# Centring the attention weights once instead of the tokens, and mask and residual of the last image on VectorE

## The chip, the core and the metric

The kernel runs on one core of a Trainium2 chip. The metric is the device time of one execution in microseconds, the median of the runs; lower is better. Five engines work side by side, each through its own list of instructions, in order: TensorE (PE, with its weight loads shown apart as PEld), VectorE (DVE), ScalarE (ACT), GpSimd (POOL), and SyncE (SP), which here only issues DMA transfers. An instruction that waits for another engine holds up everything behind it on its own engine.

## The reference

Four images of 384 channels and 32 x 32 pixels go through two layers. All of it is float32.

```python
# layer 0: x + conv(groupnorm(x)); four directional scans, merged, layer norm, gelu
x = x + _L0_conv_ref(_gn(x), ...)
t = _to_tokens(x)                                   # (4, 1024, 384)
t = t + _L1_attn_ref(_ln_t(t), Wq, Wk, Wv)          # causal attention, one head of 384
t = t + _L1_ffn_ref(_ln_t(t), gate_w, ..., b2)      # 4 experts, the best 2 count

def _ln_t(v, eps=1e-5):
    m = jnp.mean(v, axis=-1, keepdims=True)
    s = jnp.var(v, axis=-1, keepdims=True)
    return (v - m) / jnp.sqrt(s + eps)
```

The attention is softmax(q k^T / sqrt(384)) v with q, k and v linear in the normed tokens. A mean taken off the tokens can therefore be taken off the weights: with J the matrix that averages over channels, (v - m) W equals v (I - J) W.

## The kernel before, in words

Channels lie on the 128 partitions in M = 3 groups, tokens along the free dimension (L = 1024). An image is worked off in two stages.

*Scan stage.* Image b has 192 units (`IMAGE`), 768 over the four images. A unit is one selective scan over 1024 tokens on 128 partitions: ACT makes `da` by an exponential (L551), DVE multiplies `v` = du x B (L558) and runs the scan `h` (L564), POOL multiplies `h` by C (L571), and every four units PE sums them into `y` (L596, "row"). For part of image 0, `v` comes from PE instead (L841).

*Token stage.* When the last row of an image is in, `evict` (L616) forms `yb`, and `finish` does a layer norm on it (`layernorm`, names ending in `l0`), the gelu (L857) and the residual (L862). Then `behind` runs `attention` and `experts`. Attention loads two weights, wg = Wq Wk^T scaled (made once by `fold` after image 0 and kept in DRAM as `g_d`) and wv, norms the tokens to `axn`, and makes `qt` (pq, L896) and `vt` (pv, L907). For every block of 128 queries it then makes `scores` (ss, L925, with the causal mask added by an identity matmul, L930), `softmax` (L939 to L955), `turn` (transposes tp, L970) and, for every two blocks, `values` (po, L991, with the residual `yb` added by an identity matmul, L988). A copy by ACT brings the result back into `yb` (L1003), and a DMA stores it. `experts` is 8 rounds (two halves of the tokens, four experts) of 36 + 36 float32 matmuls of 512 columns, ph (L1182) and fy (L1207); the profile counts each float32 matmul as two instructions.

*What sets the order.* The program is written out by hand, tick by tick. The last loop of the kernel gives one unit to each tick, up to tick 767, and goes on without units until all is done. Within a tick the order is: functions that are due (`defer`), `v` of this tick's unit (`front`), POOL's product (`back`), functions due `inner`, then one step of every parked generator (`unpark`), then the scan (`middle`), then `go_on`. In `go_on` the generators in `side` (`fold`, `finish`, the norms ahead of the experts) may each go on by about one microsecond's worth of PE work, and then the first of `waiting` (attention and experts of one image) as far as a budget reaches: `pace` microseconds are added to `spare` in each tick, 4.4 in attention and 3.3 in the experts, and every yield of `"pe", n` takes n off. `"wait", n` pauses a generator for n ticks, and `"inner"` moves it ahead of the scan of the next tick. Matmul results go to PSUM banks handed out by `banks` (four of them), and buffers of one image row to `slots` (eight).

*The attention's layer norm* in `layernorm` (L626 to L705, names ending in `at`): PE takes the mean with the full `mean_w` (mu, L639), which leaves it on all partitions; DVE subtracts it (L652) from `yb` into `axn`; ACT squares (L664); PE averages the squares with 32 columns of `mean_w`, four blocks of 128 tokens side by side in the array (var, L671); ACT takes the root (L679), DVE the reciprocal (L684), PE spreads it over the partitions (rb, L690), and DVE multiplies (L700). `axn` lies in pool `a0`, which has one buffer: the accumulator of the experts of the image before (`fx`) lies there too, so the subtraction waits until that image is `stored`.

In ticks: image 0's rows end so that `finish` starts at tick 195, `fold` is done at 204, the attention begins at 206 and its norm is over at 210. Image 1: attention from 398, experts of image 0 written out by 396. Image 2: from 590, norm over at 595, experts of image 1 written out by 589. Image 3: from 782, experts of image 2 written out by 780.

Of the kernel before, what the change touches and what calls it, by code (L numbers as in the profile page):

```python
# [8 lines left out]
F32 = mybir.dt.float32  # L9
AF = mybir.ActivationFunctionType  # L10
ALU = mybir.AluOpType
# [4 lines left out]
P = 128  # L16
B = 4
# [32 lines left out]
def hybrid_kernel(  # L50
# [120 lines left out]
        for b in range(B) for h in range(NH)  # L171
    }
    g_d = dram.tile([P, M, C], F32, tag="g", name="g_d")


    def load_image(b):
# [446 lines left out]
            waiting.append(behind(b))  # L623


    def layernorm(dst, src, name, lag, b=0, into=None):  # L626

# [6 lines left out]
        for h in range(n):  # L636
# [4 lines left out]
                )  # L641
            mus.append(mu)
            yield "pe", 2.6
        if into is not None:
            while b > 0 and b - 1 not in stored:

                yield "wait", 1
            dst = into()
        yield "inner", 0
        for h in range(n):  # L650
            s = bass.ts(h, 512)
# [46 lines left out]
        for h in range(n):  # L698
# [3 lines left out]
                ALU.mult,  # L702
            )
            banks.give(f"rb_{name}_{h}")
        return dst  # L705

    folded = []

    def fold():

        def square(name):
            t = pools["ht"].tile([P, M, L], F32, tag="ht", name=name)
            t = t.rearrange("p m l -> p (m l)")[:, : 2 * M * C]
            return t.rearrange("p (j c d) -> p j c d", j=2, c=M)

        raw = square("w_raw")
        for j, w in enumerate((wq, wk)):  # L720
            nc.sync.dma_start(raw[:, j], w.rearrange("(c p) d -> p c d", p=P))
        wt = square("w_t")
        yield "wait", 2
        for j in range(2):
            for d in range(M):
                ps = yield from banks.take(f"pwt_{j}_{d}")
                for c in range(M):
                    nc.tensor.transpose(
                        ps[:, c * P : (c + 1) * P], raw[:, j, c, d * P : (d + 1) * P], ident
                    )  # L730
                yield "wait", 1
                nc.scalar.copy(wt[:, j, d, :], ps[:, :C])
                banks.give(f"pwt_{j}_{d}")
        g = square("g_s")[:, 0]
        for m in range(M):
            ps = yield from banks.take(f"pg_{m}")
            for d in range(M):
                nc.tensor.matmul(
                    ps[:, :C], wt[:, 0, d, m * P : (m + 1) * P], wt[:, 1, d, :],
                    start=(d == 0), stop=(d == M - 1),  # L740
                )
            yield "wait", 1
            nc.scalar.activation(g[:, m, :], ps[:, :C], AF.Copy, scale=-scale)
            banks.give(f"pg_{m}")
        yield "wait", 1
        nc.sync.dma_start(g_d, g)
        folded.append(1)


# [97 lines left out]
    def finish(b):  # L847
# [8 lines left out]
        for m in range(M):  # L856
# [9 lines left out]

            defer(1 + m // 2, add)

    def attention(b, yb, fx0):
        while not folded:  # L870
            yield "wait", 1
        gw_ = []
        for name, w in ((f"wg_{b}", g_d), (f"wv_{b}", wv.rearrange("(c p) d -> p c d", p=P))):
            ta = yield from slots.take(f"{name}a", P, 2, C)
            nc.sync.dma_start(ta, w[:, :2, :])
            tb = yield from slots.take(f"{name}b", P, C)
            nc.sync.dma_start(tb, w[:, 2, :])
            gw_.append((ta[:, 0, :], ta[:, 1, :], tb))
        xn = yield from layernorm(
            None, yb, f"at_{b}", 0, b,  # L880
            lambda: pools["a0"].tile([P, M, L], F32, tag="a0", name=f"axn_{b}"),
        )
        qt = pools["ht"].tile([P, M, L], F32, tag="ht", name=f"qt_{b}")
        vt = pools["ht"].tile([P, L // P, C], F32, tag="ht", name=f"vt_{b}")

# [33 lines left out]
        def scores(i):  # L919
            ss = []  # L920
            for o in range(0, (i + 1) * P, 512):
                e = min((i + 1) * P, o + 512)
                ps = yield from banks.take(f"ss_{b}_{i}_{o}")
                for c in range(M):
                    nc.tensor.matmul(  # L925
                        ps[:, : e - o], qt[:, c, i * P : (i + 1) * P], xn[:, c, o:e],
                        start=(c == 0), stop=(c == M - 1 and e <= i * P),
                    )
                if e > i * P:
                    nc.tensor.matmul(ps[:, e - o - P : e - o], ident, causal, start=False, stop=True)  # L930
                ss.append((o, e, ps[:, : e - o]))
                yield "pe", 2.6 * (e - o) / 512
# [2 lines left out]

        def softmax(i, ss, pr):
            nb = sm.tile([P, 4], F32, tag="nb", name=f"nb_{b}_{i}")
            for n, (o, e, ps) in enumerate(ss):
                nc.vector.tensor_reduce(nb[:, n : n + 1], ps, AX.X, ALU.min)  # L939
            if len(ss) == 2:  # L940
# [38 lines left out]
        def values(step):  # L979
# [3 lines left out]
            for m in range(M):  # L983
# [1 line left out]
                    names.append(f"po_{b}_{step}_{m}")  # L985
                    po = yield from banks.take(names[-1])
                pv = po[:, (m % 2) * TQ : (m % 2 + 1) * TQ]
                nc.tensor.matmul(pv, ident, yb[:, m, s], start=True, stop=False)  # L988
                for j in range(nj):
                    o = max(0, j - 2 * step) * P  # L990
                    nc.tensor.matmul(  # L991
                        pv[:, o:], vt[:, j, m * P : (m + 1) * P], pts[step][j // 4][:, j % 4, o:],
                        start=False, stop=(j == nj - 1),
                    )
                if m % 2 == 0:
                    pos.append(po)
# [3 lines left out]
            def add():  # L1000
                for m in range(0, M, 2):
                    n = min(2, M - m)
                    nc.scalar.copy(  # L1003
                        yb[:, m : m + n, s],
                        pos[m // 2][:, : n * TQ].rearrange("p (m t) -> p m t", m=n),
                    )
                banks.give(*names)
                nc.sync.dma_start(t2_d[b][:, :, s], yb[:, :, s])
                if step == 1:
# [389 lines left out]
```

## Time and profile before

| | |
|---|---|
| median of 3 runs | 3795.2 us (3794.46 to 3797.17) |
| the profiled execution | 3795.0 us, of which the span of the profile is 3793.2 us |
| mean granted clock of TensorE | 0.927 |
| DVE busy / PE busy / ACT busy | 2964.4 / 3366.5 / 2089.9 us |
| last scan ends | 3121.8 us |
| first pq matmul of the last image | 3186.6 us |
| first expert matmul of the last image | 3283.4 us |

Up to about 3122 us the scans of the four images run, from about 690 us on with the attention and the experts of the image before beside them on PE. From 3122 us on only the last image's token stage is left, behind the rest of image 2's experts. Times in a timeline are microseconds from the span's start; in brackets stands the idle time of the engine ahead of the instruction and what ended it.

### The profile page before, as it was taken

The numbers are of one execution on the slowest core, as the hardware profiler recorded it, in microseconds if no ns is written. First come the engines' busy times: TensorE is split into PE (matmuls) and PEld (weight loads), VectorE is DVE, ScalarE is ACT, GpSimd is POOL, SyncE is SP. The second block draws the span as 40 slices with busy tenths as digits, with TensorE's granted clock in tenths as the row PEclk, the third lists the DMA queues.
The fourth block names the chain that finished last, engine by engine and source line by source line (L and its number), as shares of the span: only waits on it lengthen the run. The fifth ranks groups of instructions, "written<-read, shape, count | busy, mean of one in ns | idle before, by whom it ended". The sixth has DMA issues, their size and how long they took to land.

```text
span 3793.2 us, 34275 instructions
## 1 busy us (share of the span) xinstructions
PE 3366.5 (89%) x11543; PEld 1518.3 (40%) x11543; DVE 2964.4 (78%) x2084; ACT 2089.9 (55%) x2767; POOL 1815.1 (48%) x776
## 2 busy tenths in 40 slices
PE   4666666689999999799999999889999999999999
PEld 1333333245333334345333343354343434644444
DVE  6899899998889999989998999999999982210000
ACT  5888888555656656556655555455554552422121
POOL 2777777554455556445555565455665550000000
PEclk7767877799999999898999999899999999999999
DMA  6655655635576767336666565345656551222321
GB/s 207 218 209 219 220 199 208 230 122 184 191 245 208 255 205 251 140 136 225 215 221 223 197 212 185 143 167 195 215 194 237 180 182 38 91 78 80 96 83 53
DMA packets 407983, 678.80 MB, mean 179 GB/s; under 512 B 33488, under 2 KB 280576, under 8 KB 407808
## 3 DMA queue, kind: packets, MB, share of 16 engines
q1 hardware_dynamic: 401600, 676.22, 52.0%
q8 instruction: 91, 1.49, 0.2%
q10 hardware_dynamic: 6208, 0.39, 0.1%
q14 instruction: 84, 0.69, 0.1%
HBM read 604.57 MB, written 71.96 MB: 178 GB/s over the span
## 4 chain that ended last, share of the span: by engine, by line
DVE 42%; PE 40%; ACT 7%; issue 6%; DMA 3%; POOL 1%; DVEq 0%; SPq 0%; POOLq 0%; ACTq 0%
DVE h L564 25%; PE ph L1182 13%; PE fy L1207 13%; DVE v L558 12%; PE y L596 4%; ACT da L551 2%; PE ss L925 2%; PE pq L896 2%; PE pv L907 2%; PE v L841 1%; PE pxd L391 1%; ACT st L819 1%; DVE du L438 1%; DMA du<-dts 1%; PE po L991 1%
## 5 line engine op out<-in xcount | busy, mean ns | idle before, releaser
L571 POOL TENSOR_TENSOR h<-h,bc 128x1024 f32<-128x1024 f32 x768 | 1814.0, 2366 | 1308.6 <-DVE v L558 1142.8
L564 DVE TENSOR_TENSOR_SCAN h<-da,v 128x1024 f32<-128x1024 f32 x768 | 1750.5, 2284 | 104.4 <-PE v L841 29.7
L551 ACT ACTIVATE da<-dt,a 128x1024 f32<-128x1024 f32 x768 | 883.3, 1156 | 923.7 <-DVE h L564 887.2
L1182 PE MATMUL ph<-fx,w 128*128 128x512 f32 x2304 | 1024.8, 601 | 6.5 <-ACT dt L430 2.3
L1207 PE MATMUL fy<-ht,w 128*128 128x512 f32 x2304 | 1021.2, 600 | 1.5 <-ACT dt L430 0.9
L558 DVE TENSOR_TENSOR v<-du,bc 128x1024 f32<-128x1024 f32 x678 | 841.7, 1241 | 38.8 <-DMA du<-dts 21.7
L1182 PEld LDWEIGHTS ph<-fx,w 128*128 128x128 f32 x2304 | 434.9, 192 | 583.4 <-issue 528.9
L1207 PEld LDWEIGHTS fy<-ht,w 128*128 128x128 f32 x2304 | 436.8, 192 | 574.9 <-issue 552.2
L596 PE MATMUL y<-h,sel 128*32 128x512 f32 x3072 | 493.8, 661 | 101.4 <-POOL h L571 101.3
L1167 ACT ACTIVATE ht<-ph,b1s 128x512 f32<-128x512 f32 x384 | 257.2, 678 | 459.5 <-PE ph L1182 459.1
L1216 DVE SCALAR_TENSOR_TENSOR fy<-fy,b2s,tw 128x512 f32<-128x512 f32 x96 | 72.4, 754 | 425.8 <-PE fy L1207 425.8
L596 PEld LDWEIGHTS y<-h,sel 128*32 128x32 f32 x3072 | 97.4, 116 | 412.2 <-issue 219.8
L841 PE MATMUL v<-ident,st 128*128 128x128 f32 x720 | 143.1, 364 | 110.6 <-DVE h L564 110.6
L819 ACT ACTIVATE st<-turn,bt 128x128 f32<-128x128 f32 x736 | 213.6, 532 | 0.1
L841 PEld LDWEIGHTS v<-ident,st 128*128 128x128 f32 x720 | 115.4, 189 | 155.6 <-DVE h L564 78.3
L1171 ACT ACTIVATE ht<-ht 128x3072 f32<-128x3072 f32 x64 | 176.9, 2763 | 0.8
L551 ACT ACT_TABLE_LOAD x108 | 138.6, 1283 | 13.8 <-DMA dt<-dts 11.9
L991 PE MATMUL po<-pt,vt 128*128 128x256 f32 x480 | 105.4, 368 | 9.4 <-ACT pt L887 9.4
L424 PE MATMUL pdt<-xd,wdt 12*128 12x512 f32 x184 | 81.0, 762 | 34.8 <-ACT dt L430 19.4
L925 PE MATMUL ss<-axn,qt 128*128 128x512 f32 (+3 forms) x288 | 106.1, 514 | 0.8 <-ACT pr L943 0.5
L991 PEld LDWEIGHTS po<-pt,vt 128*128 128x128 f32 x480 | 93.1, 195 | 24.9 <-ACT pt L887 12.0
L939 DVE TENSOR_REDUCE nb<-ss 128x1 f32<-128x512 f32 (+3 forms) x48 | 26.1, 554 | 78.8 <-PE ss L930 63.5
(200 smaller groups left out, 1661.7 us busy)
## 6 DMA issues: line engine op xcount, KB each, us to landing
bc<-rows SPq DMA_DIRECT2D x384, 512.0 KB, 4.9
w<-in_w SPq DMA_DIRECT2D x384, 384.0 KB, 6.1
dt<-dts SPq DMA_DIRECT2D x192, 512.0 KB, 3.8
du<-dts SPq DMA_DIRECT2D x192, 512.0 KB, 6.7
dts<-dt SPq DMA_DIRECT2D x48, 512.0 KB, 5.3
dts<-du SPq DMA_DIRECT2D x48, 512.0 KB, 3.8
fx<-t2d SPq DMA_DIRECT2D x12, 768.0 KB, 5.3
tw<-mkd SPq DMA_DIRECT2D x32, 256.0 KB, 6.3
```

The source lines that it names most:

```text
L551: nc.scalar.activation(u["da"], spread["dt4", n], AF.Exp, scale=a4[:, g, u["q"] : u["q"] + 1])
L558: return nc.vector.tensor_tensor(u["v"], spread["du4", n], spread["bc", n][:, 0, :], ALU.mult)
L564: nc.vector.tensor_tensor_scan(u["h"][:, ::step], u["da"][:, ::step], u["v"][:, ::step], 0.0, op0=ALU.mult, op1=ALU.add,)
L571: product = nc.gpsimd.tensor_tensor(h, h, spread["bc", n][:, 1, :], ALU.mult)
L596: nc.tensor.matmul(y, sel, h, start=first, stop=last, tile_position=(0, jj * DJ))
L819: nc.scalar.activation(st[:, 4 * h + t, :].rearrange("p (d i) -> p i d", i=NI)[:, i, :], ps[h][:, t * P : (t + 1) * P], AF.Copy, scale=bt[ ...
L841: nc.tensor.transpose(u["v"][:, t * P : (t + 1) * P], st[:, t, u["j"] * P : (u["j"] + 1) * P], ident)
L925: nc.tensor.matmul(ps[:, : e - o], qt[:, c, i * P : (i + 1) * P], xn[:, c, o:e], start=(c == 0), stop=(c == M - 1 and e <= i * P),)
L991: nc.tensor.matmul(pv[:, o:], vt[:, j, m * P : (m + 1) * P], pts[step][j // 4][:, j % 4, o:], start=False, stop=(j == nj - 1),)
L1167: nc.scalar.activation(ht[:, f, :], ps, AF.Identity, bias=bias)
L1182: nc.tensor.matmul(ps, tiles[n][:, c, (f % 2) * P : (f % 2 + 1) * P], xns[h][:, c, :], start=(c == 0), stop=(c == M - 1),)
L1207: nc.tensor.matmul(pss[m], tiles[n][:, f, :], hts[fh][:, f, :], start=(fh == 0 and f == 0), stop=(fh == 1 and f == FH - 1),)
```

## The change

Four parts. (1) `fold` centres the three weights: two small matrices, `centre[1]` = I - J's own block and `centre[0]` = the block beside it, take the place of the identity in the transposes, so that each block of a transposed weight is a sum of three matmuls; wv is loaded, centred by nine matmuls, and kept in DRAM as `wv_d`. (2) The attention's norm becomes `scaled_tokens`: squares and means are taken of the tokens as they are, both means with the 32-column form, the variance is the difference, and only one multiplication from `yb` into `axn` is left. The wait for `stored` moves behind the statistics. (3) For the last image (`alone`) DVE adds the mask to the scores in PSUM in place of PE's identity matmul. (4) For the last image DVE adds the attention's result onto `yb`, in place of PE's identity matmul and ACT's copy.

```diff
     def fold():
+        extra = pools["a0"].tile([P, M, L], F32, tag="a0", name="w_extra")
+        extra = extra.rearrange("p m l -> p (m l)")
+        vs = extra[:, : 2 * M * C].rearrange("p (j c d) -> p j c d", j=2, c=M)
+        centre = extra[:, 2 * M * C : 2 * M * C + 2 * P].rearrange("p (j d) -> p j d", j=2)
+        nc.sync.dma_start(vs[:, 0], wv.rearrange("(c p) d -> p c d", p=P))
+        for same in range(2):
+            nc.vector.scalar_tensor_tensor(
+                centre[:, same, :], ident, float(same), mean_w, ALU.mult, ALU.subtract
+            )
...
                 for c in range(M):
-                    nc.tensor.transpose(
-                        ps[:, c * P : (c + 1) * P], raw[:, j, c, d * P : (d + 1) * P], ident
-                    )
+                    for o in range(M):
+                        nc.tensor.matmul(
+                            ps[:, c * P : (c + 1) * P], raw[:, j, o, d * P : (d + 1) * P],
+                            centre[:, int(o == c), :], start=(o == 0), stop=(o == M - 1),
+                        )
...
         nc.sync.dma_start(g_d, g)
+        for m in range(M):
+            ps = yield from banks.take(f"pwv_{m}")
+            for c in range(M):
+                nc.tensor.matmul(
+                    ps[:, :C], centre[:, int(c == m), :], vs[:, 0, c, :],
+                    start=(c == 0), stop=(c == M - 1),
+                )
+            yield "wait", 1
+            nc.scalar.copy(vs[:, 1, m, :], ps[:, :C])
+            banks.give(f"pwv_{m}")
+        yield "wait", 1
+        nc.sync.dma_start(wv_d, vs[:, 1])
         folded.append(1)
...
+    def scaled_tokens(b, yb):
+        sqs = []
+        for c in range(M):
+            sq = yield from slots.take(f"sq_at_{b}_{c}", P, L)
+            nc.scalar.activation(sq, yb[:, c, :], AF.Square)
+            sqs.append(sq)
+        var = yield from banks.take(f"var_at_{b}")
+        for o, src in ((NH * P, [yb[:, c, :] for c in range(M)]), (0, sqs)):
+            for h in range(NH):
+                for c in range(M):
+                    for q in range(4):
+                        k = h * 512 + q * P
+                        nc.tensor.matmul(
+                            var[32 * q : 32 * (q + 1), o + h * P : o + (h + 1) * P],
+                            mean_w[:, :32], src[c][:, k : k + P],
+                            start=(c == 0), stop=(c == M - 1), tile_position=(0, 32 * q),
+                        )
+                yield "pe", 1.0
+        slots.give(*[f"sq_at_{b}_{c}" for c in range(M)])
+        rs = one.tile([P, NH, P], F32, tag=f"rs{NH}", name=f"rs_at_{b}")
+        flat = rs.rearrange("p h t -> p (h t)")
+        nc.scalar.activation(flat, var[:, NH * P : 2 * NH * P], AF.Square)
+        yield "inner", 0
+        nc.vector.tensor_tensor(flat, var[:, : NH * P], flat, ALU.subtract)
+        banks.give(f"var_at_{b}")
+        nc.scalar.activation(rs, rs, AF.Sqrt, bias=eps)
+        yield "wait", 1
+        nc.vector.reciprocal(rs, rs)
+        backs = []
...
+        while b > 0 and b - 1 not in stored:
+            yield "wait", 1
+        xn = pools["a0"].tile([P, M, L], F32, tag="a0", name=f"axn_{b}")
+        yield "inner", 0
+        for h in range(NH):
+            s = bass.ts(h, 512)
+            nc.vector.tensor_tensor(
+                xn[:, :, s], yb[:, :, s], backs[h].unsqueeze(1).to_broadcast([P, M, 512]), ALU.mult
+            )
+            banks.give(f"rb_at_{b}_{h}")
+        return xn
...
     def attention(b, yb, fx0):
+        alone = b == B - 1
...
-        xn = yield from layernorm(
-            None, yb, f"at_{b}", 0, b,
-            lambda: pools["a0"].tile([P, M, L], F32, tag="a0", name=f"axn_{b}"),
-        )
+        xn = yield from scaled_tokens(b, yb)
...
-                if e > i * P:
+                if e > i * P and not alone:
                     nc.tensor.matmul(ps[:, e - o - P : e - o], ident, causal, start=False, stop=True)
...
         def softmax(i, ss, pr):
+            if alone:
+                ps = ss[-1][2][:, -P:]
+                nc.vector.tensor_add(ps, ps, causal)
...
-                nc.tensor.matmul(pv, ident, yb[:, m, s], start=True, stop=False)
+                if not alone:
+                    nc.tensor.matmul(pv, ident, yb[:, m, s], start=True, stop=False)
...
-                    nc.scalar.copy(
-                        yb[:, m : m + n, s],
-                        pos[m // 2][:, : n * TQ].rearrange("p (m t) -> p m t", m=n),
-                    )
+                    y, po = yb[:, m : m + n, s], pos[m // 2][:, : n * TQ]
+                    po = po.rearrange("p (m t) -> p m t", m=n)
+                    if alone:
+                        nc.vector.tensor_add(y, y, po)
+                    else:
+                        nc.scalar.copy(y, po)
```

In the attention the second weight is read from `wv_d` instead of `wv`.

## The prediction

> **What bounds the kernel now.** I read the page's busy times and slices first, then the engines' shares by stage, then the timeline around the three places that the change touches.
>
> ```profile
> PE 3366.5 (89%) x11543; PEld 1518.3 (40%) x11543; DVE 2964.4 (78%) x2084; ACT 2089.9 (55%) x2767; POOL 1815.1 (48%) x776
> DVE  6899899998889999989998999999999982210000
> ...
> 2346.60:3130.40 783.80, 745.28 (x2549) 324.24 (x2548) 740.61 (x508) 411.09 (x436) 447.54 (x190) 0.97 0.54 185
> 3130.40:3186.60 56.20, 47.69 (x213) 22.87 (x213) 24.55 (x20) 14.97 (x20) 0.00 (x0) 0.94 0.19 64
> 3217.60:3283.40 65.80, 64.91 (x331) 49.01 (x329) 13.61 (x31) 27.10 (x59) 0.00 (x0) 1.00 0.18 59
> 3283.40:3793.20 509.80, 503.73 (x1218) 225.16 (x1217) 45.05 (x83) 117.54 (x125) 0.00 (x0) 0.99 0.27 82
> ```
>
> The last four lines give span, then busy time of PE, PEld, DVE, ACT, POOL, the granted clock and DMA. The first is image 3's scan stage: DVE 740.6 of 783.8 us. The rest is mostly gaps of 0.1 us, so DVE sets the pace; PE looks as busy, but a unit costs DVE 3.69 us, plus about 0.23 for the experts' sums (24 pairs of 0.75 + 0.69 in some 150 ticks), against 3.3 + 0.46 us of PE work per tick. The second is the start of the tail, where PE has holes, the others the last attention and experts, where PE runs with hardly a gap. So the time is DVE's up to 3122 us, the latency of a norm up to 3187, PE's from there on.
>
> Prices, with count, sum and mean in ns, then the idle time ahead:
>
> ```profile
> L652 DVE TENSOR_TENSOR axn<-yb,mu_at 128x1536 f32<-128x1536 f32 x8 | 13.7, 1749 | 3.9 <-DMA out<-fx 3.9
> L930 PE MATMUL ss<-causal,ident 128*128 128x128 f32 x64 | 12.3, 274 | 0.0
> L988 PE MATMUL po<-yb,ident 128*128 128x256 f32 x96 | 29.7, 391 | 1.0 <-ACT pr L943 0.8 <-ACT pt L887 0.2
> L728 PE MATMUL pwt<-ident,w_raw 128*128 128x128 f32 x18 | 3.6, 341 | 1.7 <-ACT w_t L732 1.5 <-DMA w_raw<-in_wq 0.2
> ```
>
> And the last image's norm on PE, then DVE:
>
> ```profile
> 3159.90 5.32 PE L1207 MATMUL fy<-ht,w 128*128 128x512 f32 x12
> 3166.55 5.97 PE L639 MATMUL mu_at<-yb,mean_w 128*128 128x512 f32 x12 [1.34 <-DVE yb L862]
> 3176.57 3.30 PE L671 MATMUL var_at<-sq_at,mean_w 128*32 128x128 f32 x48 [4.04 <-ACT sq_at L664]
> 3182.84 3.59 PE L690 MATMUL rb_at<-rs_at,ident 128*128 128x128 f32 x16 [2.98 <-DVE rs_at L684]
> 3186.57 1.98 PE L896 MATMUL pq<-axn,wg_3a 128*128 128x512 f32 x4
> ...
> 3174.09 3.42 DVE L652 TENSOR_TENSOR axn<-yb,mu_at 128x1536 f32<-128x1536 f32 x2 [3.93 <-DMA out<-fx]
> ```
>
> From `yb` complete (3168.8) to the first pq pass 17.8 us, of which DVE waits until 3174.1 for the store of image 2, whose buffer `axn` takes.
>
> **What the Trainium skill says.** "Perfetto Trace Analysis", Identifying the Most-Contended Engine, warns that matmul busy time says little of how near PE is to its limit. The trace agrees: matmul records overlap (mean 600 ns for ph), so I price PE by spacing: 72 ph passes in 30.90 us of the chain are 0.43 us each, a 128-column pass is 0.11 (two L930 passes: 0.22), a 256-column one 0.22 (two of L988: 0.43). "VectorE: DVE Perf Modes", The TRN2 errata, gives (N+151)/0.96 ns for a float32 tensor_tensor; the trace has 1749 to 1754 for N = 1536 (formula 1757) and 687 for 512 (691). I use it as an estimate where no row exists: 0.42 us for N = 256, 0.29 for 128. "TensorE: Matmul & The Clock Gate", Why this matters for your kernels, says PE-idle gaps over about 3 us halve the clock; above, 48 var passes took 3.30 us after a 4.04 us gap, while 24 of the same form took 0.86 in a busy stretch. "ScalarE: Activation LUTs", What ACT_TABLE_LOAD costs, puts a table load at 1283 ns; the page shows 1283.
>
> **Part 1, the norm in images 0 to 2 (beside scans).** DVE loses two subtractions (3.41 us back to back) and gains one of 256 columns, 0.42: -2.99. Its new wait: squares and 96 passes must be through by then. In images 1 and 2 `spare` is 3.3 when the norm begins, so four yields of 1.0 push the rest into the next tick and the subtraction comes two ticks on; no wait. In image 0 `spare` is 4.4, it comes one tick on: da 1.15 + three squares of about 1.05 (from 619 ns for 512 columns) + var's end 0.8 + square 0.47 = 5.6 us against DVE's 4.9 of scan and products, so 0.7 us of waiting, with the scan and with it POOL and `da` queued behind. Sum -2.3 - 3.0 - 3.0 = -8.3. PE loses 12 passes of 0.43 and gains 48 in 1.6: -3.6 per image, beside DVE's work, so worth nothing there. In image 2 the buffer wait leaves the front of the norm, which ends after 4 ticks instead of 5: the experts are written out by tick 779 instead of 780.
>
> **Part 2, fold.** PE: 54 matmuls of two 128-column passes, 11.9 us, for 18 one-pass transposes, 2.0; plus 9 matmuls of two 384-column passes (pg: six in 1.93 us), 5.8. Together +15.7 us between 687 and 747 us. There PE's idle pieces (the timeline's brackets, such as 4.46 us before var_l and 3.71 within a row) sum to 18 us, which covers it. ACT gets three copies of 0.49, DVE two small operations, +0.6. SP gets wv's load ahead of `w_raw`'s two (0.59 MB, about 3 us at 200 GB/s), which the first pwt waits for, with mu_l and the row behind it on PE; DVE's first subtraction of that norm now starts 6.7 us after mu_l ends, and its multiplication 2.2 us after rb_l. I put the stalls at +1.5, bounds 0 (all covered) and 18.7 (work and load laid bare). `folded` comes at 208 instead of 204, the attention two ticks later, its norm a tick shorter, so experts 0 end at 397, within the 398 at which image 1 begins; beyond that each tick would cost up to 3.7 us. The read of `wv_d` right behind its write holds SP perhaps 4 us, with fetches behind it that lead by 3 ticks (11 us) and land in 3.8 to 6.7: covered.
>
> Scan stage: -8.3 + 0.6 + 1.5 = **-6.2** (bounds 0 and -12, as the DVE's present waits for a late PE, up to 5.4 us each, shift either way when token work moves a tick against the rows).
>
> **Part 3, start of the tail.** Counted from the last row's end (3130.3 before, pq 56.3 later). With experts 2 a tick earlier, the budget gives PE this order: fy 5.15, mu_l 5.15, fy 5.15, var_l 1.6, fy 5.15, half rb_l 0.9, fy 5.15, half rb_l 0.9: 29.2, against 29.8 before, but the last fy now lies inside the chain, not behind it. DVE then has an fy pair 1.45 and the last multiplications: 33.2; table load and gelus +4.8 = 38.0; residual 39.3. PE is cold by then (10 us idle): mean passes 3.3 and var 2.9 = 45.5, subtraction 45.9, root (its table loaded meanwhile) 46.4, reciprocal 48.2, first half rb 50.0, first multiplication 51.8. That is 4.5 less. One more ph group ahead of the row may delay it by 1.5: **-3.0** (bounds +3, all of that group and a late reciprocal; -8, if PE stays warm). The store no longer matters; it ends before the multiplication.
>
> **Part 4, last attention.** PE loses 8 masks of 0.22 and 12 identities of 0.43: -6.96. DVE gets 8 x 0.29 and 4 x (0.69 + 0.42) against 13.6 us busy in 65.8, ACT loses its copies. But the mask waits for the last score block, and stands before the reductions of both: a softmax of two blocks is ready 0.6 to 0.8 us later. Before values of step 2, PE already waits 0.90 us for `pt` behind that softmax on ACT; there the gain of 0.65 turns to a loss of 0.4, and three smaller spots lose about 0.3 each: +1.9. **-5.1** (bounds -7.0 and -2). The experts behind it are PE at full rate and only shift.
>
> **Sum.** -6.2 - 3.0 - 5.1 = -14.3 on the profiled execution's 3795.0 us (span 3793.2 and 1.8 around it; the median, 3795.2, is 0.2 off): 3780.7, so **3781 us**.
>
> **Rivals.** (A) The forecast, own range 3773 to 3787; for it, DVE's continuous stretches. (B) Scan stage gives nothing: what DVE saves it waits for PE (the timeline has waits of 4.9 us for mu_ff and 5.4 for ss). 3795.0 - 3.0 - 5.1 = 3787. Against it: in 2880 to 3090 us DVE hardly waits. (C) More: waits shrink too, PE stays warm: -9 - 6.5 - 6.5 = 3773. Against it: the idle PE above. (D) Slower: fold. If PE's cover of 18 us is mostly not where the passes fall, the laid-bare 18.7 us plus one tick of 3.7 for image 1 and one of 3.7 for image 2 outweigh 16.4 of gains (14.3 with the 0.6 + 1.5 of fold's cost put back): 3795.0 + 26.1 - 16.4 = 3805. It decides from 16.4 us of fold's cost. For it: rows and mu_l stand behind pwt in PE's order; against it: seven buffers of h let scans run ahead of rows.
>
> **Numbers.** A 0.56, B 0.22, C 0.12, D 0.10. A measurement of this kernel can tell 0.2%, 7.6 us, from no change. B lies at that edge and splits. Faster: 0.53 + 0.12 + 0.11 = 0.76; same: 0.03 + 0.11 + 0.02 = 0.16; slower 0.08. Range 3769 to 3792 leaves out D and the ends of C and B.
>
> **What would show it.** Last scan ends near 3116 us instead of 3121.8; PE's first pq of image 3 some 9 us earlier than 3186.6, the first ph some 14 earlier than 3283.4, equal passes after it. Around 690 to 750 us no new DVE wait over 2 us for mu_l, rb_l or du. Wrong would be: a last scan at or behind 3122, experts of image 0 running into image 1's norm, or PE waiting for `pt` more than 4 us in the last attention.

## The result and the profile after

| | before | after |
|---|---|---|
| median of 8 runs, us | 3796.18 (3790.32 to 3803.41) | 3781.78 (3778.22 to 3784.2) |
| profiled run, us (its span) | 3795.0 (3793.2) | 3782.19 (3780.4) |
| last scan ends | 3121.8 | 3114.3 |
| last `y` pass ends | 3130.35 | 3125.58 |
| first pq pass of image 3 | 3186.57 | 3176.97 |
| first ph pass of image 3 | 3283.44 | 3272.45 |

The ratio of after to before is 0.9965 (95% interval 0.9956 to 0.9974): faster by 0.35%, about 13 us (the two medians lie 14.4 us apart). The forecast was 3781 us.

The stages of the changed kernel, in the columns used before (window and length, then busy time of PE, PEld, DVE, ACT and POOL, the granted clock, and DMA):

```profile
2342.40:3125.60 783.20, 743.75 (x2597) 327.17 (x2595) 738.50 (x507) 414.35 (x436) 447.63 (x190) 0.97 0.55 185
3125.60:3177.00 51.40, 38.70 (x237) 21.95 (x237) 21.73 (x19) 15.01 (x18) 0.00 (x0) 0.85 0.21 69
3208.90:3272.50 63.60, 60.40 (x292) 43.96 (x290) 19.20 (x47) 23.58 (x51) 0.00 (x0) 0.97 0.19 61
3272.50:3780.40 507.90, 501.96 (x1217) 223.98 (x1217) 45.06 (x83) 117.55 (x125) 0.00 (x0) 1.00 0.28 82
```

The first window is image 3's scan stage up to the last row. DVE is busy 738.5 of 783.2 us, as full as before; the stage's length is compared below by counting scans, since the left edge of this window is put by hand. The second is the start of the tail, 4.8 us shorter. The third is the last attention, where TensorE's busy time fell from 64.9 to 60.4 us but 3.2 us of idling stand beside it and the clock is 0.97, not 1.00. The fourth, the experts, is 1.8 us shorter although the same passes run in it: in before its clock was 0.99.

The start of the tail on TensorE in the timeline of the changed kernel (start, duration, then in brackets the idle time ahead and what ended it):

```profile
3147.86 1.05 PE L686 MATMUL rb_l<-rs_l,ident 128*128 128x128 f32 x8
...
3153.90 1.05 PE L686 MATMUL rb_l<-rs_l,ident 128*128 128x128 f32 x8
3160.95 0.66 PE L902 MATMUL var_at<-yb,mean_w 128*32 128x128 f32 x8 [6.00 <-DVE yb L881]
...
3166.32 2.54 PE L902 MATMUL var_at<-sq_at,mean_w 128*32 128x128 f32 x48
3173.07 3.76 PE L922 MATMUL rb_at<-rs_at,ident 128*128 128x128 f32 x16 [4.21 <-DVE rs_at L917]
3176.97 2.83 PE L968 MATMUL pq<-axn,wg_3a 128*128 128x512 f32 x4
```

One group of fy passes (5.32 us) stands between the two halves of rb_l. The second half is late, so TensorE idles 6.00 us, and 48 var passes then take 2.54 us; the second line of windows has a mean granted clock of 0.85 for this stretch. The norm's DVE work is what was priced: the subtraction takes 0.42 us, each of the two multiplications 1.75.

### The profile page after: what moved, and what is told of

The parts are those of the page before. It is cut to its first block, busy times and chain, and to the rows that moved or that the text cites. A ratio compares the mean times of both kernels' runs of the same rounds, so it can differ in the third digit from the quotient of the medians.

```text
span 3780.4 us, 34707 instructions
## 1 busy us (share of the span) xinstructions
PE 3348.6 (89%) x11755; PEld 1523.6 (40%) x11755; DVE 2962.4 (78%) x2098; ACT 2088.0 (55%) x2754; POOL 1815.4 (48%) x776
## 5 line engine op out<-in xcount | busy, mean ns | idle before, releaser
L997 PEld LDWEIGHTS ss<-axn,qt 128*128 128x128 f32 x288 | 50.5, 193 | 50.2 <-issue 30.0
```

What stands on the lines that cost most here:

```text
L997: nc.tensor.matmul(ps[:, : e - o], qt[:, c, i * P : (i + 1) * P], xn[:, c, o:e], start=(c == 0), stop=(c == M - 1 and (alone or e <= i * P)),)
```

## How to compare scan stages

The table counts from the start of the 101st scan, which comes at 380.1 to 386.1 us from run to run although the program up to there is the same everywhere; that drift belongs to no change. "Scans" is the time from there to the start of the last scan; the three columns behind it are the stages of 192 scans that carry the tokens of images 0, 1 and 2; then come three stretches of the tail: "row to pq" from the end of the last `y` pass (the row) to the first pq, "ss to ph" from the first score pass to the first expert pass, and "experts" from there to the end.

| kernel | scans | im. 0 | im. 1 | im. 2 | row to pq | ss to ph | experts | span |
|---|---|---|---|---|---|---|---|---|
| before | 2738.6 | 831.2 | 823.9 | 783.8 | 56.2 | 65.8 | 509.8 | 3793.2 |
| after | 2728.7 | 828.5 | 820.2 | 780.5 | 51.4 | 63.6 | 508.0 | 3780.4 |
| e1_fold_only | 2741.1 | 824.0 | 832.0 | 785.5 | 63.0 | 65.8 | 509.7 | 3806.1 |
| e2_norms_012 | 2728.8 | 828.7 | 820.0 | 780.6 | 55.3 | 65.8 | 509.7 | 3787.1 |
| e3_norms_all | 2728.9 | 828.8 | 819.9 | 780.5 | 51.3 | 65.8 | 509.7 | 3781.6 |
| e4_alone_only | 2735.9 | 829.0 | 823.1 | 784.1 | 56.5 | 61.9 | 508.1 | 3787.5 |
| e5_fold_double | 2736.2 | 835.8 | 819.8 | 781.0 | 51.1 | 63.6 | 508.0 | 3785.0 |
| e6_mask_late | 2728.7 | 825.7 | 820.8 | 782.5 | 51.4 | 61.0 | 511.3 | 3780.1 |
| e7_late_and_copies | 2728.9 | 828.9 | 819.9 | 780.5 | 51.3 | 60.1 | 507.9 | 3776.1 |
| e8_fold_3_ticks | 2736.4 | 826.7 | 827.1 | 783.0 | 50.8 | 63.6 | 507.9 | 3784.3 |
| e9_wait_front | 2731.5 | 828.0 | 820.5 | 783.3 | 48.4 | 63.6 | 507.9 | 3773.9 |
| e10_residual_only | 2736.1 | 830.7 | 821.8 | 781.1 | 51.1 | 62.4 | 509.7 | 3787.8 |
| e11_all | 2725.6 | 825.3 | 820.0 | 780.6 | 48.7 | 59.2 | 509.6 | 3774.1 |
| e12_fold_light | 2725.9 | 825.7 | 820.9 | 779.6 | 51.1 | 63.6 | 507.9 | 3775.3 |

Up to the last scan seven of these are the same program (after, e2, e3, e6, e7, e10, e11). They show what one profile can tell: the scans lie between 2725.6 and 2736.1 us, image 0 between 825.3 and 830.7, image 1 between 819.9 and 821.8, image 2 between 780.5 and 782.5. Before and e4 are one program as well. A difference below some 10 us in the scans, 5 us in image 0, or 2 us in images 1 and 2, is therefore read from no single profile, and the differences of scan stages below are to be taken with that spread.

## The experiments

**The parts put in one after the other.** The first three kernels rebuild the change in steps; the fourth is its last step alone on the kernel before. Centring twice gives the same as once, so the old norm can stand beside the new weights.

```diff
 # e1_fold_only (e2: the new norm "if b in (0, 1, 2)"; e3: in all images)
-        alone = b == B - 1
+        alone = False
-        xn = yield from scaled_tokens(b, yb)
+        xn = yield from centred_norm(None, yb, f"at_{b}", 0, b, lambda: ...)  # as in before
```

> The fold of the change alone: centred weights, but the norm of all four images as before (centring tokens that no longer need it changes nothing in what is computed), mask and residual on TensorE as before. Theory (the prediction's term): fold costs +2.1 us in all, the last scan ends at 3121.8 + 2.1 = 3123.9 us, ratio to before 1.0006. Rival (fold laid bare, the case in which the forecast would have been slower): +16 to +26, last scan at 3138 or later, ratio 1.004 to 1.007. A second rival (its work is all beside DVE): last scan within 1 us of 3121.8.

> Fold and the new norm in images 0 to 2; image 3 keeps the old norm, mask and residual on TensorE. Theory (additive savings of DVE work): last scan 8.3 us earlier than with the fold alone, near 3115.6, and a tail as before behind it; ratio 0.9984. Rival (part of the saving becomes waiting for PE, as the trace of the changed kernel suggests by its new waits of 6.0 and 7.7 us for du in image 0): image 0 keeps at most 2 us of its saving, the last scan comes only 5 to 7 us earlier than with the fold alone. If all of it became waiting (case B of the prediction), it would stand where the fold alone leaves it.

> The changed kernel with mask and residual of the last image left on TensorE: all four norms new. Theory: same last scan as with images 0 to 2 alone, from the last row's end to the first pq pass of image 3 51.8 us instead of 56.3, and from that pq to the first ph pass 96.9 us as in the kernel before; ratio 0.9976. Rival: the gain of the tail's start is eaten by PE standing one group of expert passes further behind the rows (the y evict waits 11 us and not 8.6), so that pq comes only 2 us earlier than with the old norm.

> The kernel before with the last image's mask and residual added by DVE, nothing else. Theory (the prediction's Part 4): first pq to first ph 91.8 us instead of 96.9, the time 5.1 us less, ratio 0.9987; scan stage unchanged to the tick. Rival (from the changed kernel's trace, where this stretch took 95.5): new waits of PE for pt and for the norm's reciprocal behind the residual on DVE give most back; 94 to 96 us, ratio 0.9992 to 0.9997.

| kernel | median, us | ratio to before (95%) |
|---|---|---|
| e1_fold_only | 3807.5 | 1.0033 (1.0020 to 1.0045) |
| e2_norms_012 | 3788.19 | 0.9982 (0.9976 to 0.9989) |
| e3_norms_all | 3785.17 | 0.9975 (0.9966 to 0.9985) |
| e4_alone_only | 3791.47 | 0.9990 (0.9982 to 0.9998) |

The fold alone makes the kernel slower by 12 us, between the first expectation and the second, and far from the third. Its scans take 2.5 us more than in before and 5.2 more than in e4. That this lies near the +2.1 confirms nothing: equal programs spread further, and the reckoning put the cost into image 0, where e1 takes 824.0 us, less than before and e4 do, while image 1 takes 832.0, some 8 us more. In the profile's 12.9 us there are also 3.2 of the drift ahead of the 101st scan. The tail has 6.8 (row to pq 63.0 instead of 56.2). Its timeline on TensorE:

```profile
3134.11 1.92 PE L597 MATMUL y<-h,sel 128*32 128x512 f32 x16
3135.97 5.42 PE L1344 MATMUL ph<-fx,w 128*128 128x512 f32 x12
...
3165.59 15.62 PE L1369 MATMUL fy<-ht,w 128*128 128x512 f32 x36
3181.04 5.31 PE L715 MATMUL mu_at<-yb,mean_w 128*128 128x512 f32 x12
...
3199.06 2.47 PE L1052 MATMUL pq<-axn,wg_3a 128*128 128x512 f32 x4
```

Three groups of fy of image 2 stand ahead of image 3's norm, where before had one. The order in which the program emits its work says why; it is fixed before the program runs, so its ticks can be counted exactly. The fold ends at tick 208 instead of 204 and image 0's norm two ticks later; its experts end at 399 instead of 396, one tick behind the 398 at which image 1's tokens are ready. The old norm waits for the store of the image before in its middle, with the rest of its chain still to come, so the delay is handed on: experts 1 end at 592 instead of 589, experts 2 at 783 instead of 780. With the new norm the ends are 396, 589, 779.

So e2 gains 19 us on e1, of which the DVE work saved is less than half: the scans fall by 12.3 us (8.3 expected) and the way from the last row to pq by 7.8, less 2.7 by which the row comes later behind the last scan. Against the mean of before and e4, image 1 and image 2 are shorter by 3.1 us each in the mean of the seven, image 0 by 2.0. The rival, that image 0 keeps at most 2 us of its saving, cannot be told from the theory in a stage that scatters by 5 us; in the others nothing is given back. e3 moves the first pq from 55.3 to 51.3 us behind the last row: theory, not rival. e4 is treated below with the attention.

**Do the fold's passes cost anything?** Every pass of the centring issued twice, then the centring left out with all ticks kept.

```diff
 # e5_fold_double: pwt are the transposed weights, pwv is wv
-                for c in range(M):
+                for c in [c for c in range(M) for _ in range(2)]:   # for pwt; the same for pwv
 # e12_fold_light
-                    for o in range(M):
-                        nc.tensor.matmul(ps[:, c * P : (c + 1) * P], raw[:, j, o, ...], centre[...], ...)
+                    nc.tensor.transpose(ps[:, c * P : (c + 1) * P], raw[:, j, c, d * P : (d + 1) * P], ident)
-            for c in range(M):
-                nc.tensor.matmul(ps[:, :C], centre[:, int(c == m), :], vs[:, 0, c, :], ...)
+            nc.tensor.matmul(ps[:, :C], ident, vs[:, 0, m, :], start=True, stop=True)
```

> The changed kernel with every pass of the fold's centring issued twice (the second overwrites the first with the same values): 54 matmuls more for the transposed weights and 9 for wv, 17.7 us of TensorE at the prediction's prices; no tick moves. Theory (the fold's passes lie under TensorE's idle time; of 687 to 757 us the changed kernel's trace still shows 18 us without a matmul): units 192 to 384 take within 2 us of the changed kernel's 828.5, ratio to before 0.9965. Rival (the prediction's own reckoning, which had 15.7 of 18 us of cover used up, and case D): 13 to 17.7 us laid bare, ratio 1.000 to 1.001.

> The changed kernel with the fold's passes undone and its ticks kept: the transposes as before, and wv copied through TensorE without centring, 13.8 us of passes less. It leaves the centring out, so that the attention's tokens keep their mean. Theory (one set of passes is covered, the second set cost 7.3 us when doubled, so cover is about 26 us): units 192 to 384 within 2 us of the changed kernel's 828.5, ratio 0.9965. Rival (the first set costs in proportion, 0.41 us per us of passes as the second did): 5.7 us less, ratio 0.9950.

With the passes doubled the kernel takes 3789.39 us, ratio 0.9985 (0.9978 to 0.9991). Image 0 takes 835.8 us, 7.3 more than in the profile of after, 7.7 more than the mean of the seven. Both expectations fell: not nothing, and not 13. The waits of DVE that appear in that stretch add up to it (timeline of e5, last bracket is the idle time ahead):

```profile
709.39 1.75 DVE L648 TENSOR_TENSOR yb<-yb,mu_l 128x1536 f32<-128x1536 f32 x1 [3.61 <-PE mu_l L640]
727.85 1.75 DVE L680 RECIPROCAL rs_l<-rs_l 128x256 f32<-128x256 f32 x1 [3.44 <-ACT rs_l L675]
```

These are the mu_l and the norm behind the pwt passes, 7.05 us, and TensorE's busy time between 687 and 757 rises from 52.0 to 64.3 us. So some 10 of the 17.7 us were still covered. With the centring left out, image 0 takes 825.7 us and the ratio is 0.9963 (0.9950 to 0.9975), against 0.9965. Two of the seven kernels with the full fold have 825.7 and 825.3 as well, so no cost of the first set of passes can be seen. The rival's 5.7 us are not in the profile, though its ratio lies at the end of the interval, and a cost of some 2 us is not excluded.

The cover was not idle time alone. Between 687 and 757 us TensorE is busy 44.7 us in e12, 52.0 in after and 64.3 in e5, at a mean granted clock of 0.72, 0.84 and 0.94. The first set of passes was priced at 13.8 us and adds 7.3, the second at 17.7 and adds 12.3: with more to do in this stretch TensorE was granted more of its clock.

**Is it lateness or work that made the fold costly?** The changed kernel, with the end of the fold reported three ticks later.

```diff
         nc.sync.dma_start(wv_d, vs[:, 1])
+        yield "wait", 3
         folded.append(1)
```

> The changed kernel with the end of the fold reported three ticks later, no work added: the experts of image 0 end at tick 399 instead of 396, behind the 398 at which image 1's tokens are ready. Theory (the fold alone lost its 12 us because each image's experts end later by ticks that the old norm, with its wait for the output's store in its middle, hands on to the next image; the new norm has that wait at its end and catches up): image 1's attention starts one tick late, image 2's none, the last scan within 4 us of the changed kernel's, tail as there; ratio 0.9965 to 0.9975. Rival (the late fold itself costs, whatever the norm): 7 us or more in the tail again, ratio 0.999 to 1.000.

It takes 3786.36 us, ratio 0.9973 (0.9963 to 0.9983), 4.6 us more than after by the medians. Experts 0 end at tick 399 as in e1, but experts 1 end at 590 and experts 2 at 779: the new norm catches up. The tail is that of after (50.8 us). The delay costs 6.9 us in image 1 and 2.6 in image 2 in this profile; the last scan came 4.7 us later than in after, by the count of scans 7.7. The theory holds for the tail. Its 4 us for the scans was somewhat too little: one tick behind the 398, priced at 3.7 us, cost 4.6 to 7.7, and the rival's loss in the tail is not there. So lateness alone costs some 5 us with the new norm, and the fold of e1 12 with the old norm, which hands the delay on.

**What is the tick in image 2 worth?** The wait for the store, and the new buffer, put back ahead of the subtraction.

```diff
         nc.scalar.activation(flat, var[:, NH * P : 2 * NH * P], AF.Square)
+        while b > 0 and b - 1 not in stored:
+            yield "wait", 1
+        xn = pools["a0"].tile([P, M, L], F32, tag="a0", name=f"axn_{b}")
         yield "inner", 0
...
             yield "pe", 1.0
-        while b > 0 and b - 1 not in stored:
-            yield "wait", 1
-        xn = pools["a0"].tile([P, M, L], F32, tag="a0", name=f"axn_{b}")
         yield "inner", 0
```

> The changed kernel with the wait for the last image's output store, and the new buffer, put back ahead of the norm's subtraction, where the old norm had it; image 2's norm then takes 5 ticks again and the experts of image 2 are written out by tick 780 instead of 779. Theory (the prediction's Part 3: that tick is what gives TensorE the order of the tail's start, and the order is what shortens it): from the last row to the first pq 55 us or more instead of 51.4, the whole +4 us, ratio 0.9975. Rival (the shorter norm itself is what shortens the tail, the tick is worth nothing): 51 to 52 us, ratio 0.9965.

Experts 2 end at 780 again, and this shortens the tail: row to pq is 48.4 us, which neither side expected. The timeline on TensorE:

```profile
3150.12 1.95 PE L686 MATMUL rb_l<-rs_l,ident 128*128 128x128 f32 x16
3151.90 5.32 PE L1285 MATMUL fy<-ht,w 128*128 128x512 f32 x12
3158.55 0.43 PE L902 MATMUL var_at<-yb,mean_w 128*32 128x128 f32 x8 [1.33 <-DVE yb L881]
...
3161.72 1.76 PE L902 MATMUL var_at<-sq_at,mean_w 128*32 128x128 f32 x48
3167.68 2.89 PE L926 MATMUL rb_at<-rs_at,ident 128*128 128x128 f32 x16 [4.20 <-DVE rs_at L921]
3170.71 2.62 PE L968 MATMUL pq<-axn,wg_3a 128*128 128x512 f32 x4
```

Both halves of rb_l run together and the fy group lies behind them, beside DVE's multiplications and the gelus. TensorE idles 1.33 us instead of 6.00, and its passes are quicker for it: 1.76 instead of 2.54 us for 48 of var, 2.89 instead of 3.76 for rb, at a mean granted clock of 0.98 between row and pq instead of 0.85. On the other hand image 2's scan stage takes 2.8 us longer than in after (0.8 longer than the longest of the seven), and the last row follows the last scan 2.7 us sooner. The net of the three, read from one profile each, is some 3 us for the later tick. The medians do not separate it from after: 3779.53 us, ratio 0.9961 (0.9947 to 0.9975).

With e2 and before this gives both norms of image 3 in both orders (row to pq, us):

| | rb_l in one piece, experts 2 end at 780 | rb_l in two, experts 2 end at 779 |
|---|---|---|
| old norm | 56.2 (before) | 55.3 (e2) |
| new norm | 48.4 (e9) | 51.4 (after) |

The new norm itself is worth 7.9 us in the order of before (56.2 to 48.4); the order that comes with it takes 3.0 of them back.

**The last attention.** In after TensorE waits 2.13 us for pt, the copies of the transposed softmax weights, where before waited 0.90. The line of before:

```profile
3258.11 2.65 PE L991 MATMUL po<-pt,vt 128*128 128x256 f32 x12 [0.90 <-ACT pt L887]
```

Three variants of the changed kernel were run: e6 puts the mask between the two reductions, e7 has the pt copies on DVE besides, and e10 keeps the residual on DVE alone.

```diff
 # e6_mask_late (e7 also: copies of pt by nc.vector.tensor_copy if alone)
-            if alone:
-                ps = ss[-1][2][:, -P:]
-                nc.vector.tensor_add(ps, ps, causal)
             for n, (o, e, ps) in enumerate(ss):
+                if alone and n == len(ss) - 1:
+                    nc.vector.tensor_add(ps[:, -P:], ps[:, -P:], causal)
                 nc.vector.tensor_reduce(nb[:, n : n + 1], ps, AX.X, ALU.min)
 # e10_residual_only: the mask's matmul stays for every image, no tensor_add of it
```

> The changed kernel with the mask's addition put between the two reductions of a softmax instead of ahead of both. Theory (the change's attention gives gain back because both reductions stand behind the mask, which waits for the last score block): the waits of TensorE for pt fall from 2.13 to 1.5 and for pr from 0.22 to 0, first ss to first ph 62.7 instead of 63.6, time 1 us less. Rival (ACT's order, not the mask's, sets the wait): 2.13 stays and nothing is gained.

> As with the later mask, and in the last image the copies of the transposed weights (pt) are made by DVE instead of ACT. Theory (the wait for pt is ACT's: two exponentials and the normalisation of block 7 stand ahead of the copies of block 5): the wait falls to 1.0 or less, first ss to first ph near 62.0, 1.5 us less than the changed kernel; ratio 0.9961. Rival (the copies queue on DVE behind the reductions and push the next norm's subtraction back, so that var_ff is late): 63 to 65 us.

> The changed kernel with the last image's mask left on TensorE and only the residual added by DVE. Theory (the mask's place costs as much as its passes bring): TensorE gives 8 x 0.22 = 1.8 us back to the mask and gets 1.2 (2.13 to 0.90) plus 0.2 of waiting for pt and pr, so that first ss to first ph is within 0.6 us of the changed kernel's 63.6, apart from where the clock falls. Rival (the mask's passes count in full): 65.4 us.

Before this is read, the clock has to be taken out. In the last attention and the experts, eleven of these fourteen kernels have one stretch of 3.4 us in which TensorE is granted 0.50; e6 has two, e4 and e7 none. Such a dip costs about 1.7 us wherever it falls (63.6 against 61.9 in the attention, 509.7 against 508.0 in the experts). In before it lies at the end of the passes for the gate of the experts (pgate), in after behind the wait for pt. Windows of before, then of after:

```profile
3326.00:3327.00 1.00, 1.00 (x8) 1.00 (x9) 0.00 (x0) 0.00 (x0) 0.00 (x0) 0.72 0.00 0
3327.00:3328.00 1.00, 1.00 (x2) 0.51 (x3) 0.52 (x3) 0.17 (x1) 0.00 (x0) 0.50 0.00 0
3328.00:3329.00 1.00, 1.00 (x3) 0.46 (x2) 0.82 (x5) 0.05 (x1) 0.00 (x0) 0.50 0.00 0
3329.00:3330.00 1.00, 1.00 (x3) 0.47 (x2) 0.86 (x5) 0.00 (x0) 0.00 (x0) 0.57 0.00 0
```

```profile
3243.57:3246.98 3.41, 1.28 (x9) 0.99 (x8) 1.97 (x3) 2.92 (x7) 0.00 (x0) 1.00 0.00 0
3246.98:3250.39 3.41, 3.41 (x11) 2.70 (x10) 0.00 (x0) 2.38 (x4) 0.00 (x0) 0.50 0.00 0
```

So a part of the attention's gain seemed lost in the attention and came back, unearned, in the experts. The 508.0 of the table are experts without the dip, 509.7 with it, 511.3 with two. e4 has it in neither stage, and its 61.9 against 65.8 of before is the clean value of mask and residual: -3.9. By its own measure, from pq to ph, e4 takes 93.0 us and lies between the theory (91.8) and the rival (94 to 96): the rival's waits are there, and they give back less than it said. TensorE works 6.2 us less (65.84 less 0.90 of waiting, against 61.92 less 3.20), and waits 2.3 more. The waits of e4 are those of after. In the timelines of e4, e7 and e11 they read:

```profile
3254.91 5.03 PE L996 MATMUL po<-pt,vt 128*128 128x256 f32 x24 [2.13 <-ACT pt L888]
3264.68 1.16 PE L690 MATMUL rb_ff<-rs_ff,ident 128*128 128x128 f32 x8 [0.61 <-DVE rs_ff L684]
```

```profile
3243.63 5.00 PE L1067 MATMUL po<-pt,vt 128*128 128x256 f32 x24 [0.69 <-DVE pt L959]
3253.38 1.16 PE L686 MATMUL rb_ff<-rs_ff,ident 128*128 128x128 f32 x8 [0.61 <-DVE rs_ff L680]
```

```profile
3240.78 5.00 PE L1071 MATMUL po<-pt,vt 128*128 128x256 f32 x24 [0.69 <-DVE pt L963]
3252.03 10.00 PE L1071 MATMUL po<-pt,vt 128*128 128x256 f32 x48 [0.35 <-DVE pt L963]
```

In e6 the wait for pt falls to 1.67 us and that for pr is gone. It takes 61.0 us from ss to ph without a dip, 0.9 below the clean 61.9 of the change's own form: the theory in direction, with 0.46 instead of 0.63 us for pt. The whole time shows nothing of it (3783.61 us, 0.9967, 0.9955 to 0.9980); in the profile two dips fall into the experts. In e7 the wait falls to 0.69 us and ss to ph takes 60.1, with no dip at all: better than the theory's 62.0, and not the rival. The kernel takes 3780.46 us, 0.9958 (0.9945 to 0.9970). In e10 ss to ph takes 62.4 us without a dip, 0.5 above the change's clean value, so of the mask's 1.8 us of passes 0.5 remain as gain. That is the theory, though TensorE's wait for pt is 1.33 us and not 0.90. The kernel takes 3781.32 us, 0.9970 (0.9959 to 0.9981).

**A version better than both.**

```diff
 # e11_all: e7, and
+        if b == B - 1:                      # in finish(), behind the norm
+            nc.scalar.activation(dump, eps, AF.Gelu)
+        if b == B - 1:                      # in scaled_tokens(), ahead of the square of the mean
+            nc.scalar.activation(dump, eps, AF.Sqrt)
-            defer(1, add)
+            defer(2 if alone and step == 2 else 1, add)
```

> A version meant to be better than both: the changed kernel with the mask late, the pt copies on DVE, the residual of step 2 one tick later (behind the reciprocal of the next norm, for which TensorE waits 0.61 us), and for image 3 the tables of Gelu and of the root loaded ahead of the moment they are needed (1.28 and 0.85 us of the chain from the last row to pq). Theory (these waits are on the path): row to pq 49.3 us instead of 51.4, first ss to first ph 59.5 instead of 63.6, time 3777; ratio 0.9950. Rival (PE's order sets the tail's start, the tables do not matter): row to pq stays at 51.3.

It takes 3776.01 us, ratio 0.9950 (0.9938 to 0.9963). That is the lowest median of all, 5.8 us below after, but its interval still overlaps those of after, e7 and e9. Row to pq is 48.7 us: the tables count, by 2.7 us where 2.1 were expected. ss to ph is 59.2 us, and the wait for rs_ff is gone (above). The order of e9 together with these edits was not tried.

## Why the prediction was right

The three terms held in kind: the scan stage, the start of the tail and the last attention each became shorter. That their sum fits to 1 us is partly luck. The scan stage gave 1.7 us more than its term, and the other two together 2.1 less.

**Scan stage, -6.2.** Measured -7.9 between the means of the same programs (2729.4 for the seven, 2737.3 for before and e4); -9.9 in the two profiles themselves. Images 1 and 2 gave 3.1 each where 3.0 were reckoned. In image 1 DVE's continuous stretches turned saved work into time: DVE is busy 762.6 us of its stage in after, 764.3 in before and 765.7 in e4. For image 2 this is less sure. In e9 DVE is spared the same work (746.7 us busy, as in after, against 748.8 in before), but with the tick put back the stage takes 783.3 us and not 780.5. So a part of image 2's gain may be the tick's; one profile does not settle it.

Image 0 gave 2.0 net, where 2.3 less 2.1 were reckoned, and not by the reckoned way. Its subtraction waits 1.54 us, not 0.7. DVE's busy time in its stage falls by 0.4 us only, from 765.45 to 765.08: two of the four small instructions that combine the two reductions of a softmax (128x1) take 1.71 and 1.30 us in after, where they took 0.18 and 0.16. The first of the two, in before and in after:

```profile
821.64 0.18 DVE L941 TENSOR_TENSOR nb<-nb 128x1 f32<-128x1 f32 x1
825.79 1.71 DVE L1016 TENSOR_TENSOR nb<-nb 128x1 f32<-128x1 f32 x1
```

In before this one follows a reduction that had to wait for its scores; in after both reductions run without a gap ahead of it. Why it then takes longer, the trace does not show. Two more waits of 6.0 and 7.7 us for du appear in image 0's stage in after, and waits of 4.8 (rb_ff) and 2.9 (pgate) vanish. Such shifts come with the moved ticks, and what remains of image 0's gain has no cause that was isolated.

**Fold, +2.1 with bounds 0 and 18.7.** The passes were hidden, but not only in the 18 us of idle pieces as argued: less 15.7 these would have left 2 us, and the doubling found some 10 left. TensorE's busy time grew by less than the price of the passes while its granted clock rose (above), which the reckoning left out. So the bound of 2 was wrong on the safe side. What the step missed further is that the ticks were the danger and not the passes: experts 0 at 397 "within the 398" (396 in the program) was the margin on which 12 us hung. The prediction named the deadline and priced a tick beyond it at up to 3.7 us; e8 shows some 5 us, and e1, where the old norm passes the delay on to every later image, 12.

**Start of the tail, -3.0.** From the last row to pq 51.4 us where 51.8 stood, in exactly the foreseen order. One more group ahead of the row made it 2.7 us later against the last scan, not 1.5, so the part came to -2.1. The step that failed is the view of the tick: an earlier end of image 2's experts was counted as part of the gain. e9's profile shows that it costs some 3 us on balance with the new norm, because the last fy group goes into the chain and TensorE then idles and slows down.

**Last attention, -5.1.** The wait for pt grew by 1.23 us, where 1.05 was reckoned, and the three smaller spots came to 1.07, where 0.9 was: 2.3 given back, against 1.9. The mis-sized term is the passes: 6.96 by spacing, 6.2 in e4. Together they leave -3.9 where -5.1 stood. One cause was not seen, the residual on DVE ahead of the reciprocal for rb_ff (0.61 us). In the profile of after the sum is veiled by the clock, so that the first ph came 11.0 us earlier and not the foreseen 14: -1.4 from pq to ph, -1.8 in the experts that were to be equal passes, and 0.85 lost ahead of the scores, where four pq passes on a cold TensorE took 2.83 us and not 1.98.

**The rivals.** B, the scan stage gives nothing, is refuted by image 1, and by image 2 if the tick is counted as part of the change. C, -22 us, is refuted too: the scan stage gave -7.9 of its -9, but the tail and the attention gave less than the forecast, not more. D's passes laid bare are not seen, but its other half, a tick lost to image 1 and to image 2, happens in e1: the attention begins at tick 399 for image 1 and at 592 for image 2, where before has 398 and 590. It did not happen in the change because the new norm is short enough and waits for the store at its end.

## What to carry to other kernels

Where work is emitted in ticks, a piece of setup is priced by the deadline of what waits for it, and by whether the next stage can catch up, before its passes are priced at all. A shorter chain can bring a worse order of other engines' work with it: compare the new chain in the old order. Before a gain of 1 or 2 us on TensorE is believed or denied, look for the stretch of half clock in both profiles. And before a difference of a few us between two profiles is explained, see how far profiles of one program lie apart: here 10 us in the scans.

## What the hardware showed unexpectedly

The granted clock falls to 0.50 although TensorE never idles for more than 2.13 us there, and where it falls looks like chance: behind the wait of 2.13 us in after but not behind the same wait in e4, and behind the 24 pgate passes (4 columns each) in before, where TensorE had no gap at all, but not behind those of after. The traces show an order in it. In all fourteen profiles the granted clock changes only at whole steps of 3.413 us, whatever the program does: in after, the stretches at 0.50 begin at 3158.24, 3171.89 and 3246.98 us, which is 4 and 22 steps apart. By these traces it matters how one step is filled. In after (windows above) the wait from 3244.17 to 3246.30 lies within one step, TensorE is busy 1.28 of 3.41 us, and the next step runs at 0.50. In e4 a boundary cuts the same wait at 3253.79:

```profile
3250.38:3253.79 3.41, 2.40 (x11) 1.15 (x9) 1.83 (x6) 2.00 (x5) 0.00 (x0) 1.00 0.00 0
3253.79:3257.20 3.41, 2.29 (x11) 2.04 (x12) 1.00 (x1) 3.39 (x7) 0.00 (x0) 1.00 0.00 0
```

Both steps are busy for two thirds, and the clock stays. The steps that the wait for pt left busy for 38% (after, e5, e8, e9, e12) were followed by a dip; those that it left busy for 51% (e6), 61% (e10), 67% and 70% (e4) were not. The pgate passes count as busy in the profile, yet when 22 to 24 of them begin in one step a dip follows (before, e1, e2, e3, e6, e10, e11), and with 20 or fewer none does; 21 went both ways (e6, e3). Why passes of four columns act like idle time, no run shows.

The Trainium skill, "TensorE: Matmul & The Clock Gate", What's actually happening, ties the cold state to an idle window of about 3.4 us. Here the steps have that length, but a step did not have to be idle: one with 1.28 us of work was enough, and one full of passes with four columns.
